# The first scale and shift of an AdaLN block: from rows that are folded and turned to channels made at once

## The chip, the core and the metric

The kernel runs on one core of a Trainium2 chip. The metric is the device time of one execution in microseconds. The kernel before was run three times and takes 1318.79 us in the median (1311.11 to 1322.47).

## What is computed

The reference is one transformer block with adaptive layer norm: a conditioning vector `c` of each of four batch entries makes six vectors of 512 channels, which scale, shift and gate two branches. The first branch is a gated delta rule (a linear attention with a short convolution), the second a gated feed-forward. Everything is float32, x is 4 x 512 x 512.

```python
mod = (silu(c) @ wmod).reshape(4, 6, 1, 512)          # c: 4 x 512, wmod: 512 x 3072
sa, ca, ga, sb, cb, gb = (mod[:, i] for i in range(6))
ga, gb = (sign(g) * maximum(abs(g), 0.25) for g in (ga, gb))   # sign(0) = 1
h = layernorm(x) * (1 + ca) + sa
x = x + ga * attn(h)      # q, k, v projections, convolutions of 4 taps, delta rule, gate, Wo
h = layernorm(x) * (1 + cb) + sb
x = x + gb * ffn(h)       # silu(h @ w_gate.T) * (h @ w_up.T) @ w_down.T
```

The change concerns only the making of `sa` and `ca` (the first shift and scale, j = 0 and j = 1 in the code).

## The kernel before

The kernel is one function, `adaln_block`, written in a tile framework that schedules the recorded instructions on each engine, allocates buffers by tag, and puts in the semaphores. Activations are kept with channels on the partitions (four blocks of 128 channels, `KD = 4`) and the 512 tokens of one batch entry along the free side, so that a scale and a shift by channel are one number per partition. The work runs batch entry by batch entry: batch 0 first goes through normalisation (`first_normed_t`), keys, queries, values, gates and the delta rule, with the others following behind it, and the feed-forward of each entry is laid beside the delta rule of later ones.

**What happens first.** Two of the six column blocks of `w_mod` are loaded at once: j = 1 (scale) and j = 0 (shift), each a tile `wm` of 128 partitions x 4 x 512 (partition and second index together are the 512 rows of the contraction). Each is loaded in two halves of the contraction, k = 0, 1 by the ACT queue and k = 2, 3 by the SP queue (`early_load`, line 175). SP issues `c_in`, then x of batch 0 in two transfers, then the second halves, then the first key weight. ACT makes `sc_t`, the silu of `c` (line 188). `sc_t` is 32 columns wide with 4 used, the rest zero.

**How scale and shift are made.** `modulation_part` (line 209) takes `sc_t` as the fixed side of the matmul and a whole row of 512 columns of `wm` as the moving side. Each of the four blocks of the contraction writes its own strip of 32 partitions of one PSUM bank `pm` (line 213), so the four partial sums stand one above the other. ACT copies the bank to SBUF (`part`, line 216). `modulation_turned` (line 221) then takes each 128-column block of `part` as the fixed side and `fold`, a matrix of four stacked 32x32 identities, as the moving side: this adds the four strips and puts channels on the partitions, into a slice of the bank `scratch` (line 226). ACT writes it to `mod_t` (line 228), adding 1 for the scale. The other modulation vectors (j = 2 to 5) go the same way later, with DVE in ACT's place.

**How they are used.** `first_normed_t` (line 296) makes the statistics of batch 0 on DVE, normalises the four token chunks in place (line 309), transposes 16 blocks of 128x128 on TensorE into four banks `pxt` (line 313), and applies scale and shift on the way out of PSUM, alternately on ACT (line 320) and DVE (line 318), into `ht`. The first key projection `pp_k` (line 478) and the decay projection `pab` (line 370) read `ht`.

**What sets the order.** Each engine works through its instructions in the recorded order after scheduling. TensorE's order around the change is: the four `pm` matmuls of j = 1, one of j = 0, the four folds of j = 1, three `pm` of j = 0, six transposes, the four folds of j = 0, ten transposes, then `pp_k`. A float32 matmul that isn't a transpose shows as two LDWEIGHTS and two MATMUL records, and is counted so below; a transpose shows as one of each. The PSUM tags are `fill` (three banks), `seq` (three banks) and `scratch` (two banks, used in turns). The three `seq` allocations at the start are the fourth `pxt` bank, then `pm` for j = 1 and for j = 0; `pab` comes next and reuses the first.

Of the kernel before, what the change touches and what calls it, by code (L numbers as in the profile page):

```python
# [9 lines left out]
AF = mybir.ActivationFunctionType  # L10
# [5 lines left out]
P = 128  # L16
B, T, D = 4, 512, 512
# [6 lines left out]
KD = D // P  # L24
# [13 lines left out]
def adaln_block(  # L38
# [23 lines left out]
    vec, act, pool, pe, sp = nc.vector, nc.scalar, nc.gpsimd, nc.tensor, nc.sync  # L62
# [12 lines left out]
    def bank(tag, n, name):  # L75
        return ps.tile([P, 512], F32, tag=tag, bufs=n, name=name)

    def fill(name):
        return bank("fill", 3, name)
# [4 lines left out]
    def prep(n):  # L84


        turn[0] ^= 1
        return scratch[:, :, turn[0], :n]

    def seq(name):  # L90
        return bank("seq", 3, name)
# [13 lines left out]
    sc_t = const.tile([P, KD, S], F32, name="sc_t")  # L105
# [12 lines left out]
    mod_t = const.tile([P, 4, KD, B], F32, name="mod_t")  # L118
    MOD = {0: 0, 1: 1, 3: 2, 4: 3}
# [13 lines left out]
    start = const.tile([P, 2, NT, C + 1], F32, name="start")  # L133
# [37 lines left out]
    early = []  # L171
# [36 lines left out]

    def modulation_part(j, wm):

        pm = (seq if j < 2 else fill)(f"pm{j}")
        for k in range(KD):
            pe.matmul(pm[k * S : (k + 1) * S, :], sc_t[:, k, :], wm[:, k, :], start=True, stop=True)
        part = pa_.tile([P, D], F32, tag="acc", bufs=4, name=f"part{j}")
        if j < 2:
            act.copy(part, pm)
        else:
            vec.tensor_copy(part, pm)
        return part

    def modulation_turned(j, part):
        pt = (prep(KD * B)[:, 0] if j < 2 else fill(f"pmt{j}")[:, : KD * B]).rearrange(
            "p (t b) -> p t b", b=B
        )
        for t in range(KD):
            pe.matmul(pt[:, t, :], part[:, t * P : (t + 1) * P], fold[:, :B], start=True, stop=True)
        if j < 2:
            act.activation(mod_t[:, MOD[j]], pt, AF.Identity, bias=1.0 if j == 1 else 0.0)
        else:
            vec.tensor_scalar_add(mod_t[:, MOD[j]], pt, 1.0 if j == 4 else 0.0)  # L230

    def modulation(j, wm):
        part = modulation_part(j, wm)
        if j in MOD:
            return modulation_turned(j, part)
        pg = fill(f"pmg{j}")[:B, :]
        pe.matmul(pg, fold[:, :B], part, start=True, stop=True)
        val = pa_.tile([P, D], F32, tag="acc", bufs=4, name=f"val{j}")[:B]
        vec.tensor_copy(val, pg)
        mag = pa_.tile([P, D], F32, tag="acc", bufs=4, name=f"mag{j}")[:B]  # L240
        vec.scalar_tensor_tensor(mag, val, -1.0, val, ALU.mult, ALU.max)
        vec.tensor_scalar(val, val, 0.0, 2.0, ALU.is_ge, ALU.mult)
        vec.tensor_scalar_add(val, val, -1.0)
        vec.scalar_tensor_tensor(mag, mag, 0.25, val, ALU.max, ALU.mult)
        pool.dma_start(gate_d[j // 3], mag)
# [23 lines left out]
    for i in range(2):  # L269
# [14 lines left out]
        t = stat.tile([P, H, C], F32, name=f"xs{i}")  # L284
# [6 lines left out]
    def statistics(pool_, xt, mv):  # L291
        st = pool_.tile([P, vec.BN_STATS_DIM], F32, tag="st", bufs=2, name="st")
        vec.bn_stats(st, xt)
        vec.bn_aggr(mv, st)

    def first_normed_t(xts):

        mv = pa_.tile([P, NT, vec.BN_AGGR_DIM], F32, tag="mv", name="mv0")
        rstd = pa_.tile([P, NT], F32, tag="rstd", name="rstd0")
        pts = [(fill if k < 3 else seq)(f"pxt0_{k}") for k in range(KD)]  # L300

        for j, wm in early:
            modulation_turned(j, modulation_part(j, wm))
        for c in range(NT):
            statistics(pa_, xts[c], mv[:, c, :])
        act.activation(rstd, mv[:, :, 1], AF.Sqrt, bias=eps)
        vec.reciprocal(rstd, rstd)
        for c in range(NT):
            vec.tensor_scalar(
                xts[c], xts[c], mv[:, c, 0:1], rstd[:, c : c + 1], ALU.subtract, ALU.mult  # L310
            )
            for k in range(KD):
                pe.transpose(pts[k][:, c * P : (c + 1) * P], xts[c][:, k * P : (k + 1) * P], ident)
        ht = pa_.tile([P, KD, T], F32, tag="ht", bufs=3, name="ht0")
        for k in range(KD):
            shift, scale = (mod_t[:, i, k, 0:1] for i in range(2))
            if k % 2:
                vec.tensor_scalar(ht[:, k, :], pts[k], scale, shift, ALU.mult, ALU.add)
            else:
                act.activation(ht[:, k, :], pts[k], AF.Identity, bias=shift, scale=scale)  # L320
        return ht
# [642 lines left out]


    hts, xts = {0: first_normed_t(xts)}, {}
    keys([0], hts)
    rest = list(range(1, B))
# [93 lines left out]
```

## Time and profile before

| What | Value |
|---|---|
| Runs before, median (lowest to highest) | 1318.79 us (1311.11 to 1322.47) |
| Execution that was profiled, its own time | 1315.23 us |
| Span of its trace | 1313.5 us, 18027 instructions |
| TensorE matmul busy (PE) | 1242.2 us, 95% |
| TensorE weight load busy (PEld, overlaps PE) | 777.2 us, 59% |
| DVE / ACT / POOL busy | 713.9 / 386.3 / 249.3 us |
| First `pm` matmul | 5.50 us after the start |
| First `ht` activation | 20.32 us |
| First `pp_k` matmul | 21.14 us |

The times are microseconds from the start of the span. A row of a group of instructions reads: line, engine, operation, output <- inputs, shapes, count, and then durations. Matmuls are pipelined: each is listed from its start to its end, and neighbours overlap, so the rate of a row of matmuls is the distance between their starts and not the length of one. The chain of waits is followed back from the last instruction, at each step to what released it.

### The profile page before, as it was taken

Reading aid. Unit: us, or ns where it says so; the run is one execution under the profiler, and the core shown is the slowest. Engines: PE = TensorE matmul, PEld = TensorE weight load, DVE = VectorE, ACT = ScalarE, POOL = GpSimd, SP = SyncE. Lnnn points to the kernel's source line nnn. Section 1 sums busy time; section 2 is a strip of 40 time slices with the busy share of each in tenths; the row PEclk is TensorE's granted clock in tenths of the full one; section 3 lists DMA queues with packets and bytes.
Section 4 is the critical chain, followed back from the end, with each engine's and each line's share of the span. In section 5 each row is a group of like instructions: output and inputs, shape, how many; then the busy total and the mean of one; then the engine's idle time right before and its main releaser. Section 6 shows DMA issues by size and latency. Waiting matters only on the chain.

```text
span 1313.5 us, 18027 instructions
## 1 busy us (share of the span) xinstructions
PE 1242.2 (95%) x6620; PEld 777.2 (59%) x6620; DVE 713.9 (54%) x1547; ACT 386.3 (29%) x740; POOL 249.3 (19%) x299
## 2 busy tenths in 40 slices
PE   6899898899999998989999999899999999999998
PEld 3444355444444565757757666676666577576665
DVE  4767765555288245774445558644464444444443
ACT  3643346643142344211103332110234211011110
POOL 4210223543200012020021121011111201111111
PEclk9889999999999999999999999899999999999999
DMA  5979647767955447664335455443622243354331
GB/s 154 267 186 285 200 119 227 186 213 225 276 165 161 118 108 184 204 178 134 126 115 163 124 124 164 134 144 101 185 78 71 94 144 116 117 189 143 117 112 64
DMA packets 213271, 204.06 MB, mean 155 GB/s; under 512 B 95032, under 2 KB 163640, under 8 KB 213184
## 3 DMA queue, kind: packets, MB, share of 16 engines
q1 hardware_dynamic: 191408, 167.14, 44.6%
q0 software_dynamic: 4096, 20.99, 4.2%
q10 hardware_dynamic: 17680, 14.78, 3.5%
q8 instruction: 53, 0.87, 0.3%
q14 instruction: 34, 0.28, 0.1%
HBM read 152.94 MB, written 46.78 MB: 152 GB/s over the span
## 4 chain that ended last, share of the span: by engine, by line
PE 66%; DVE 13%; DMA 9%; POOL 4%; issue 3%; ACT 2%; SPq 1%; POOLq 0%; ACTq 0%; DVEq 0%
PE phg L927 15%; PE pd L899 15%; PE phu L927 11%; PE pwo L803 5%; PE pp_v L478 3%; PE pp_g L478 2%; PE pm L762 2%; DVE ti L660 2%; DVE tip L656 2%; PE scratch L689 2%; DMA wsum<-wsu 1%; PE pf L753 1%; DMA wsum<-wsg 1%; PE pp_k L478 1%; DMA wsg<-in_w_gate_t_dram 1%
## 5 line engine op out<-in xcount | busy, mean ns | idle before, releaser
L899 PE MATMUL pd<-wdn,hid 128*128 128x512 f32 x512 | 225.5, 593 | 0.0
L905 POOL TENSOR_TENSOR xm<-xm,tmpf 128x512 f32<-128x512 f32 x64 | 81.3, 1270 | 451.9 <-DVE tmpf L904 451.9
L899 PEld LDWEIGHTS pd<-wdn,hid 128*128 128x128 f32 x512 | 97.7, 191 | 109.2 <-issue 102.6
L927 PE MATMUL phg<-hf,wg 128*128 128x256 f32 x512 | 138.6, 388 | 0.3 <-DMA wg<-wsum 0.3
L927 PEld LDWEIGHTS phg<-hf,wg 128*128 128x128 f32 x512 | 96.4, 193 | 21.4 <-issue 7.3
L927 PE MATMUL phg<-hs,wg 128*128 128x256 f32 x384 | 103.4, 389 | 4.4 <-DVE hid L934 4.3
L927 PE MATMUL phu<-hf,wu 128*128 128x256 f32 x384 | 99.9, 384 | 2.1 <-DMA wu<-wsum 2.0
L904 DVE TENSOR_TENSOR tmpf<-pd,gb 128x512 f32<-128x512 f32 x64 | 44.1, 689 | 104.0 <-PE pd L899 93.0
L927 PE MATMUL phu<-hs,wu 128*128 128x256 f32 x384 | 96.1, 384 | 3.5 <-DVE up L940 3.5
L478 PE MATMUL pp_v<-ht,wv 128*128 128x512 f32 x192 | 93.6, 632 | 4.5 <-DVE v L561 2.3
L932 ACT COPY hid<-phg 128x256 f32<-128x256 f32 x32 | 11.9, 371 | 288.8 <-PE phg L927 286.5
L803 PE MATMUL pwo<-wo,ot 128*128 128x512 f32 x192 | 93.3, 617 | 0.0
L478 PE MATMUL pp_g<-ht,wg 128*128 128x512 f32 x192 | 91.4, 618 | 1.6 <-issue 1.6
L927 PEld LDWEIGHTS phu<-hs,wu 128*128 128x128 f32 x384 | 72.4, 191 | 22.0 <-DVE up L940 9.0
L927 PEld LDWEIGHTS phg<-hs,wg 128*128 128x128 f32 x384 | 71.6, 194 | 18.3 <-DVE hid L934 5.8
L927 PEld LDWEIGHTS phu<-hf,wu 128*128 128x128 f32 x384 | 71.3, 191 | 15.0 <-issue 5.2
L478 PEld LDWEIGHTS pp_v<-ht,wv 128*128 128x128 f32 x192 | 36.9, 202 | 46.2 <-issue 43.4
L488 DVE SCALAR_TENSOR_TENSOR acc_v<-pp_v,conv_v,acc_v 128x511 f32<-128x511 f32 (+2 forms) x72 | 53.3, 743 | 8.8 <-ACT acc_v L486 8.1
L478 PEld LDWEIGHTS pp_g<-ht,wg 128*128 128x128 f32 x192 | 35.1, 195 | 38.2 <-issue 37.0
L956 ACT ACTIVATE hid<-hid 128x1024 f32<-128x1024 f32 x32 | 33.8, 1057 | 79.9 <-DVE hid L940 63.5
L762 PE MATMUL pm<-r,l 128*128 128x128 f32 x384 | 52.7, 283 | 1.0 <-ACT r L758 0.8
L803 PEld LDWEIGHTS pwo<-wo,ot 128*128 128x128 f32 x192 | 34.4, 192 | 30.1 <-issue 28.3
(236 smaller groups left out, 1812.8 us busy)
## 6 DMA issues: line engine op xcount, KB each, us to landing
wdn<-in_w_down_t_dram SPq DMA_DIRECT2D x32, 512.0 KB, 4.3
wg<-wsum SPq DMA_DIRECT2D x32, 512.0 KB, 3.7
wu<-wsum SPq DMA_DIRECT2D x32, 512.0 KB, 3.6
wg<-wsum SPq DMA_DIRECT2D x32, 384.0 KB, 4.3
wu<-wsum SPq DMA_DIRECT2D x32, 384.0 KB, 4.4
wsum<-wsg POOLq DMA_DIRECT2D x8, 896.0 KB, 4.0
wsum<-wsu POOLq DMA_DIRECT2D x8, 896.0 KB, 4.5
wg<-in_w_g_dram SPq DMA_DIRECT2D x24, 256.0 KB, 3.2
```

The costliest lines, as they stand in the source:

```text
L478: pe.matmul(pp, w[:, k, :], ht[:, k, :], start=(k == 0), stop=(k == KD - 1))
L488: vec.scalar_tensor_tensor(acc[:, i:], pp[:, : T - i], taps[:, col, TAPS - 1 - i : TAPS - i], acc[:, i:], ALU.mult, ALU.add,)
L656: vec.tensor_tensor(v, pm[:, j, j + 1 :, None].broadcast_to([n, m, j]), t[:, j : j + 1, :j].broadcast_to([n, m, j]), ALU.mult,)
L660: vec.tensor_add(t[:, j + 1 :, :j], t[:, j + 1 :, :j], v)
L689: pe.matmul(pv[:, u, 2 * par : 2 * par + 2, :], kc[i][us, p, par : par + 2, :], qc[i][us, p, par : par + 2, :], start=True, stop=True,)
L762: pe.matmul(pm[:, h], l[:, hs.start + h, 2 * par : 2 * par + 2, :], r[:, par, hs.start + h], start=True, stop=True,)
L803: pe.matmul(pw, ot[:, h, :], wo[:, h, :], start=(h == 0), stop=(h == H - 1))
L899: pe.matmul(pd, hids[q, i // 2][:, i % 2, c * P : (c + 1) * P], wdn[q, i // 2][:, i % 2, :], start=(i == 0), stop=(i == NQ - 1),)
L904: vec.tensor_mul(tmp, pd, gb)
L905: pool.tensor_add(xm[c], xm[c], tmp)
L927: pe.matmul(o, l[:, k], r[:, k], start=k == 0, stop=k == 1)
L956: act.activation(hid, hid, AF.Silu)
```

## The change

Scale and shift are no longer made as rows, copied, folded and turned. For each block of 128 output channels the 128x128 block of `wm` is the fixed side and the four used columns of `sc_t` are the moving side, so the result has channels on the partitions at once, 128 x 4 for each block, and the contraction is summed in PSUM. This is done by halves of the contraction in the order in which they are loaded: first half of the scale, first half of the shift, second half of the scale, second half of the shift, eight matmuls each. The results go straight to `mod_t` by ACT. The later modulation vectors keep the old way; their branches for j < 2 are dropped from the two functions.

```diff
     def modulation_part(j, wm):
-        pm = (seq if j < 2 else fill)(f"pm{j}")
+        pm = fill(f"pm{j}")
         for k in range(KD):
             pe.matmul(pm[k * S : (k + 1) * S, :], sc_t[:, k, :], wm[:, k, :], start=True, stop=True)
         part = pa_.tile([P, D], F32, tag="acc", bufs=4, name=f"part{j}")
-        if j < 2:
-            act.copy(part, pm)
-        else:
-            vec.tensor_copy(part, pm)
+        vec.tensor_copy(part, pm)
         return part
 
     def modulation_turned(j, part):
-        pt = (prep(KD * B)[:, 0] if j < 2 else fill(f"pmt{j}")[:, : KD * B]).rearrange(
-            "p (t b) -> p t b", b=B
-        )
+        pt = fill(f"pmt{j}")[:, : KD * B].rearrange("p (t b) -> p t b", b=B)
         for t in range(KD):
             pe.matmul(pt[:, t, :], part[:, t * P : (t + 1) * P], fold[:, :B], start=True, stop=True)
-        if j < 2:
-            act.activation(mod_t[:, MOD[j]], pt, AF.Identity, bias=1.0 if j == 1 else 0.0)
-        else:
-            vec.tensor_scalar_add(mod_t[:, MOD[j]], pt, 1.0 if j == 4 else 0.0)
+        vec.tensor_scalar_add(mod_t[:, MOD[j]], pt, 1.0 if j == 4 else 0.0)
...
     def first_normed_t(xts):
...
-        for j, wm in early:
-            modulation_turned(j, modulation_part(j, wm))
+
+        pms = [seq(f"pmt{j}")[:, : KD * B].rearrange("p (t b) -> p t b", b=B) for j, _ in early]
+        for k in (0, KD // 2):
+            for (j, wm), pt in zip(early, pms):
+                for t in range(KD):
+                    for i in range(k, k + KD // 2):
+                        pe.matmul(
+                            pt[:, t, :], wm[:, i, t * P : (t + 1) * P], sc_t[:, i, :B],
+                            start=(i == t == 0), stop=(i == t == KD - 1),
+                        )
+                if k:
+                    act.activation(mod_t[:, MOD[j]], pt, AF.Identity, bias=1.0 if j == 1 else 0.0)
```

In the changed program TensorE's order is the 32 new matmuls in the order above, then the 16 transposes without a break, then `pp_k` as before. ACT's order is the same less the two copies; the orders of DVE, POOL and SP are the same.

## The prediction

> **What bounds the kernel now.** I read the page first, then the chain of waits over the first 60 us, then the instructions of the tiles that the change touches, and last the granted clock by stretches. On the page TensorE leads the chain that ends last:
>
> ```profile
> PE 66%; DVE 13%; DMA 9%; POOL 4%; issue 3%; ACT 2%; SPq 1%; POOLq 0%; ACTq 0%; DVEq 0%
> ```
>
> The change lies in the first 21 us. There the chain of waits (start, length, what; both in us) runs through every piece that is edited:
>
> ```profile
> 2.35 8.23 DMA wm<-in_w_mod_dram
> ...
> 10.62 1.95 PE pm L213 x5
> ...
> 12.59 0.59 ACT part L216
> ...
> 13.32 1.84 PE scratch L226 x8
> 15.16 1.86 PE pm L213 x6
> 17.02 1.47 PE pxt L313 x6
> 18.49 0.90 PE scratch L226 x8
> 19.39 0.94 PE pxt L313 x8
> 20.34 0.77 ACT ht L320
> ...
> 21.14 1.98 PE pp_k L478 x4
> ```
>
> So a microsecond won or lost before 21.14 us is one on the chain. After it nothing in the chain waits for a fixed moment: the loads it meets later (x from 37.48 to 42.21) are issued behind finished activations, so they move along. The weights for the first projections landed early enough: SP issued the last of them at 14.55 us, they land some 4.4 us after issue, and the timeline shows it idle between 15.6 and 26.96 us. I pass the shift at 21.14 to the end one to one.
>
> The second view is the landing of the four half blocks of `w_mod` (issue rows, then issue to landing):
>
> ```profile
> L179 ACTq DMA_DIRECT2D wm<-in_w_mod_dram x2: 493/512/532, 0.8 to 1.3; - x2
> L179 SPq DMA_DIRECT2D wm<-in_w_mod_dram x2: 614/750/886, 2.4 to 3.3; - x2
> DMA to landing us min/median/max: 4.5/7.6/8.7
> ```
>
> The scale's first half landed at 0.8 + 4.5 = 5.3; the ACT queue's median of 5.7 puts the other of its two at 6.9, so the shift's first half came at 1.3 + 6.9 = 8.2. The second halves came at 10.58 (the chain) and at 3.3 + 8.7 = 12.0.
>
> The third view is the price of one load-and-multiply step, from two windows of the fold into `scratch` (start 13.2 to 15, then after 18.3) and two of the transposes:
>
> ```profile
> L226 PEld LDWEIGHTS scratch<-fold,part x8: 285/333/334, 13.3 to 14.7; 128*128 128x128 f32 x8
> L226 PE MATMUL scratch<-fold,part x8: 344/354/355, 13.3 to 14.8; 128*128 128x4 f32 x8
> ...
> L226 PE MATMUL scratch<-fold,part x7: 252/253/354, 18.4 to 19.1; 128*128 128x4 f32 x7
> ...
> L313 PE MATMUL pxt<-ident,xt x6: 421/421/477, 16.9 to 18.1; 128*128 128x128 f32 x6
> ...
> L313 PE MATMUL pxt<-ident,xt x10: 272/272/306, 19.2 to 20.3; 128*128 128x128 f32 x10
> ```
>
> The same instruction takes 354 ns before and 253 ns after some 18.5 us. The clock records begin at 18.60 us and say full speed from there; the column PEclk prints 1.00 before them too, but the durations show that TensorE ran at the lower clock until then. Eight steps of the fold took 1.84 us, so their spacing at the lower clock is (1.84 - 0.354) / 7 = 0.212 us; ten transposes at the full one took 1.29 us, (1.29 - 0.272) / 9 = 0.113 us. Both load 128 columns per step, and the moving side hardly counts.
>
> The fourth view asks what raises the clock (columns: stretch, its length, then busy time of PE, PEld, DVE, ACT, POOL, granted clock, DMA share, GB/s; the two rows below are the timeline's):
>
> ```profile
> 45.91:49.32 3.41, 3.41 (x20) 2.10 (x20) 2.67 (x7) 1.31 (x3) 0.41 (x2) 0.50 1.13 193
> 49.32:52.73 3.41, 3.41 (x5) 1.33 (x4) 1.39 (x3) 0.26 (x1) 0.54 (x1) 0.50 1.20 240
> ...
> 45.94 1.02 PE L504 MATMUL pn_k<-sel,sq_k 128*64 128x2 f32 x16
> 46.90 2.92 PE L478 MATMUL pp_q<-ht,wq 128*128 128x512 f32 x3
> ```
>
> The clock changes on a grid of 3.41 us. The stretch from 45.91 had TensorE busy throughout, but 1.02 us of it with matmuls of two moving columns, and the clock stayed at one half; the next, all 512-column matmuls, was followed by full speed at 52.73. Weight loading with almost nothing streamed does not seem to count.
>
> **The change, part by part.** *Removed:* 16 steps of `pm` (8 matmuls of two passes), 16 of the fold, and the two ACT copies to `part` (0.59 us each, the first on the chain). From 10.62 to the 13th transpose, whose end starts `ht`, the old chain spends 9.7 us. *Added:* 4 groups of 8 matmuls, two passes each as in the fold, so 64 steps, each a 128x128 load and four moving columns: the form of the fold row exactly. The instruction orders of DVE, POOL and SP are the same before and after; ACT loses only the copies. The two result banks are again two of the three `seq` banks, and `pab` reuses the same first one. The wait for `ident` moves to the first transpose, and POOL made that by 1.7 us. The two `mod_t` activations (0.18 us) remain; the last comes some 2.5 us before `ht`, hidden behind the transposes, and would cost 0.18 without that cover. DVE's normalised rows are done at 13.98, which is no limit below.
>
> Now the sum at the lower clock. The first group starts, as `pm` did, at 5.47 us. Each group is 16 x 0.212 = 3.4 us: ends at 8.9, 12.3, 15.6 and 19.0. No half block is late (8.2 against 8.9, 10.6 against 12.3, 12.0 against 15.6), so TensorE waits nowhere, which is why its own rate sets the time and earlier data buy nothing. Queued behind the groups are the 16 transposes, and DVE and ACT wait for these. The 13th starts at 19.0 + 12 x 0.212 = 21.6 and ends 0.42 later, 22.0; `ht` takes 0.77 and the issue gaps 0.06: the first projection starts at 22.85 instead of 21.14, +1.7 us.
>
> Next the clock. If it is raised at 22.01, the next line of the old grid, this is all. The stretch 18.60 to 22.01 would hold 3.0 us of transposes (88%); against it, in the old run 15.19 to 18.60 had 3.1 us of wide matmuls and transposes (91%) and was followed by the raise, while 45.91 with some 70% was not. If it comes one line later, at 25.43, the projections run at half rate for 2.6 us: 1.3 us more, +3.0. Neither row decides, and 88% is nearest the one that raised it, though the grid's phase need not repeat, so I take the middle: **+2.4 us**. The page's execution took 1315.23 us by its own time (span 1313.5), which gives 1317.6; the median of the runs shown is 3.6 us higher, which gives 1321.2, rounded to **1321**.
>
> [...]
>
> **Rivals.** *The groups raise the clock.* For it: they occupy TensorE without a gap from 5.47 us, and the stretch before 18.60 that raised it held 0.5 us of folds. Against it: 45.91, and the stretch 11.77 to 15.19, where 1.8 us of folds did not raise it (though with an idle gap of 0.77). By the grid, 8.36 to 11.77 would be the first full stretch: 30 steps done, 34 left at 0.113, end at 15.6; the 13th transpose starts at 17.0, ends at 17.2, and the projection begins at 18.05: -3.1 us, 1315.7 by the median. With a kinder phase the bound is the last landing, 12.0 + 16 x 0.113 = 13.8, or -5.
>
> *The shift is lost.* The kernel has eleven more spells of half clock between 45.9 and 831 us, 51 us together, each costing half its length. Moving all work against the grid by 2 us can add or drop one or two of 3.41 us (1.7 us each), and swallow the change: 1318.8. For it: three runs of one kernel spread over 11.4 us. Against it: nothing in the chain soaks it up by itself. To move the time by over 1% (13.2 us, about what a measurement of this kernel can tell from no change) eight such spells would have to come or go; a small chance on either side.
>
> *The steps don't overlap.* All eight matmuls of a group add into few columns, two by two into the same four. If each step had to finish before the next began, it would cost 0.333 + 0.354 = 0.69 us, 64 of them 44 us, ending at 49.4 instead of 19.0: +33 us in all, 1352. It decides from 0.38 us per step on, where the whole loss passes 13.2 us. Against it: in the fold, two passes into the same four columns already follow at 0.212.
>
> **How the numbers follow.** The lower clock throughout the groups 0.67; the groups raise it 0.17; shift lost 0.09; steps that don't overlap 0.03; clock spells beyond 1% 0.04, split evenly. The time is the first case's. The range takes in -5 at the low side and +3.0 at the high side about the median, and some 4 us of run spread, which the low run (1311) and the high run (1322) show: 1312 to 1327. Within 1%: the first three, less 0.03 for spread at the edges, 0.90. Slower: 0.03 + 0.02 + 0.01 = 0.06. Faster: 0.02 + 0.02 = 0.04.
>
> **What would show it.** Right: the new matmuls run from 5.5 to about 19 us in an even row, 0.21 apart, without a wait for `w_mod` beyond the first; matmul length 354 ns; the first `pp_k` near 22.9; the first clock record at 21.5 or later. Wrong: steps of 0.11 us before 15 us and a clock record near 12 (first rival), a gap in the row before the third or fourth group, or a `pp_k` start after 30 us.

## The result and the profile after

The changed kernel takes 1324.05 us in the median, the kernel before on the same chip 1318.04: a ratio of 1.0048 [1.0029, 1.0068]. It is half a per cent slower; the forecast was 1321 and "within 1%". The profiled execution of after took 1323.99 us (span 1322.3), that of before 1315.23 (span 1313.5).

The chain of waits of after, first 30 us (start, length, what; in us), and the two rows of the tile `pmt` (count, min/median/max in ns, first and last start, shape):

```profile
0.81 4.24 DMA c_in<-in_c_t_dram
5.06 0.22 ACT sc_t L188
5.29 0.09 issue
5.38 13.78 PE pmt L300 x64
19.16 2.89 PE pxt L315 x13
...
22.14 0.79 ACT ht L322
...
22.97 2.09 PE pp_k L480 x4
```

```profile
L300 PEld LDWEIGHTS pmt<-sc_t,wm x64: 285/333/333, 5.3 to 18.7; 128*128 128x128 f32 x64
L300 PE MATMUL pmt<-sc_t,wm x64: 343/354/355, 5.4 to 18.8; 128*128 128x4 f32 x64
```

The 64 steps are one unbroken piece, 13.78 / 64 = 0.215 us each, with no wait for a half of `w_mod` inside it: the chain no longer holds the 8.23 us of `wm<-in_w_mod_dram` and begins with the load of `c_in` and `sc_t`. A weight load takes 333 ns to the last step, as in the slow fold of before (192 once the clock was raised), so the lower clock lasted through all of them; the first clock record of after stands at 23.22 us. The first projection starts at 22.97 instead of 21.14 (+1.83). By the first `pat` (the fold of the decay projection, a few matmuls behind) it is 26.95 against 25.02.

At the end the profiled pair is 8.8 us apart, though. The engines' shares of the chain on the page hardly differ (66% TensorE before):

```profile
PE 67%; DVE 13%; DMA 9%; POOL 4%; issue 4%; ACT 2%; SPq 1%; POOLq 0%; ACTq 0%; DVEq 0%
```

So the start came out as forecast against the page of before, and what had to be explained was the rest.

### The profile page after: what moved, and what is told of

It reads as the page before. It is cut to its first block, busy times and chain, and to the rows that moved or that the text cites. A ratio compares the mean times of both kernels' runs of the same rounds, so it can differ in the third digit from the quotient of the medians.

```text
span 1322.3 us, 18088 instructions
## 1 busy us (share of the span) xinstructions
PE 1253.8 (95%) x6652; PEld 792.8 (60%) x6652; DVE 712.2 (54%) x1547; ACT 385.5 (29%) x738; POOL 249.5 (19%) x299
## 4 chain that ended last, share of the span: by engine, by line
PE 67%; DVE 13%; DMA 9%; POOL 4%; issue 4%; ACT 2%; SPq 1%; POOLq 0%; ACTq 0%; DVEq 0%
PE pd L901 14%; PE phg L929 14%; PE phu L929 11%; PE pwo L805 5%; PE pp_g L480 4%; PE pp_v L480 3%; PE pm L764 2%; DVE ti L662 2%; PE scratch L691 2%; DVE tip L658 2%; PE pp_k L480 2%; PE pf L755 1%; PE scratch L734 1%; DVE acc_v L490 1%; PE pmt L300 1%
## 5 line engine op out<-in xcount | busy, mean ns | idle before, releaser
L764 PEld LDWEIGHTS pm<-r,l 128*128 128x128 f32 x384 | 49.6, 200 | 8.3 <-ACT r L760 3.5
```

Of the source, the lines that this page charges most:

```text
L764: pe.matmul(pm[:, h], l[:, hs.start + h, 2 * par : 2 * par + 2, :], r[:, par, hs.start + h], start=True, stop=True,)
```

## The experiments

Ratios are to the kernel before on the same chip, with 95% intervals. "Growth" is measured in the traces: how much later DVE's, ACT's and GpSimd's instructions come, counted from the first `pat`, than in the profiled run of before, at 210 to 220 us behind `pat` less the same at 160 to 170 us (the median over the instructions there).

**1. The kernel before, once more.** No edit.

> The kernel before, unchanged, for the spread of its runs and for a second trace. The traces so far put 1.9 us of the 8.8 us between the two profiled executions before the first key projection, and 6.8 us into spells of half clock after it (51 us of them in the trace of before, 65 us of after). Theory that the later spells are more often met by the changed kernel: ratio 1.000 within 0.002, and a mean granted clock near 0.980 over its runs, against 0.9768 over the 19 runs of the changed one (0.003 of 1320 us is 4 us of half clock, 2 us of time). Theory that the later spells were luck of the two profiled executions: the same mean clock of 0.977 here, so that the 6 us between the medians must lie before the first record of the clock. The first raise of the clock need not come at 18.6 us again: if the grid lies otherwise, at 22 to 26 us.

Ratio 0.9986 [0.9962, 1.0011]; growth -0.3 us. The mean granted clock of its runs is 0.982, that of the runs of the changed kernel 0.977, so the later spells of half clock were not just luck of the two profiled executions. But its start isn't that of the page. From the timeline of this run (start, length, engine, line, what):

```profile
18.25 1.71 PE L226 MATMUL scratch<-fold,part 128*128 128x4 f32 x8
19.82 2.37 PE L313 MATMUL pxt<-ident,xt 128*128 128x128 f32 x10
22.48 3.07 PE L478 MATMUL pp_k<-ht,wk 128*128 128x512 f32 x4 [0.29 <-ACT ht L320]
...
27.44 0.97 PE L386 MATMUL pat<-fold,ab 128*128 128x32 f32 x8
```

The last ten transposes take 2.37 us here and took 1.29 on the page: the clock was raised at 24.69 us, not at 18.60. The page of before, from which I had 21.14, had an early line of the clock's grid (the clock records of that trace, all but the last, which the end of the trace cuts off, are 3.41 us long or multiples of it). A third trace of the same work (experiment 7) has `pp_k` at 22.43 and `pat` at 26.70. Against the mean `pat` of these three, 26.4, four traces of the changed kernel and its repeats (26.95, 26.90, 27.71, 27.87) stand at 27.4: the start costs about 1.0 us, not 1.9.

**2. Do weight loads raise the clock?** The moving side of the groups is repeated 32 times, to 128 columns; the weights and the number of steps stay.

```diff
-  pms = [seq(f"pmt{j}")[:, : KD * B].rearrange("p (t b) -> p t b", b=B) for j, _ in early]
+  pms = [seq(f"pmt{j}").rearrange("p (t n b) -> p t n b", n=S, b=B) for j, _ in early]
...
-      pt[:, t, :], wm[:, i, t * P : (t + 1) * P], sc_t[:, i, :B],
+      pt[:, t], wm[:, i, t * P : (t + 1) * P],
+      sc_t[:, i, None, :B].broadcast_to([P, S, B]),
...
-      act.activation(mod_t[:, MOD[j]], pt, AF.Identity, bias=1.0 if j == 1 else 0.0)
+      act.activation(mod_t[:, MOD[j]], pt[:, :, 0], AF.Identity, bias=1.0 if j == 1 else 0.0)
```

> The changed kernel, with the four moving columns repeated 32 times to 128, so that each step still loads 128 columns and now streams 128 as well; the extra results are not read. Theory that only streamed columns raise the clock: the steps stay 0.21 us apart until the first line of the grid behind a full stretch of 3.41 us, between 8.8 and 12.3 us, then fall to 0.11 us; the groups end at 14 to 16 us instead of 19.2, and the first key projection starts at 17 to 19 us instead of 22.97: 4 to 6 us less than the changed kernel, about 3 less than before, ratio 0.996 to 0.999. Theory that the clock follows the time since TensorE began, whatever it streams: no change, first raise at 22 us or later, ratio 1.004 to 1.006. Theory that a step costs by its streamed columns: 128 columns for four make it slower, ratio above 1.01.

The scheduler also moved the gates' exponential and `pab` ahead, so a second version ties that exponential's scale to a small tile `one` that DVE makes behind `ht`; ACT, GpSimd and SP then keep the changed kernel's order, and only `pab` stays ahead of `pp_k`. A third version repeats only 8 times, to 32 columns, and needs no such tile. The second is shown against the changed kernel, the third against the first version.

```diff
-            act.activation(neg_a, neg_a, AF.Exp)
+            one = pa_.tile([P, 1], F32, tag="one", bufs=1, name="one")
+            vec.tensor_scalar(one, hts[0][:, KD - 1, 0:1], 0.0, 1.0, ALU.mult, ALU.add)
+            act.activation(neg_a, neg_a, AF.Exp, scale=one)
```

```diff
-  pms = [seq(f"pmt{j}").rearrange("p (t n b) -> p t n b", n=S, b=B) for j, _ in early]
+  pms = [seq(f"pmt{j}")[:, : KD * 8 * B].rearrange("p (t n b) -> p t n b", n=8, b=B) for j, _ in early]
...
-      sc_t[:, i, None, :B].broadcast_to([P, S, B]),
+      sc_t[:, i, None, :B].broadcast_to([P, 8, B]),
```

> The wide-sided variant again. There the scheduler, expecting wider matmuls to take longer, had put the exponential of neg_a and its table load ahead of the first ht activations, and moved parts of the first key and query stages; here that exponential takes its scale from a tile of ones that DVE makes behind ht (one more DVE instruction of about 0.2 us), so ACT, SP and POOL have the order of the changed kernel again, and only pab stays ahead of pp_k. Theory that this reordering ate the 4 to 6 us that the wide side won at the start: ratio 0.9950 to 0.9975. Theory that the gain is lost later whatever the order: 0.9985 to 1.0010, as the wide side had.

> The changed kernel with 32 moving columns (the four, eight times) instead of 4 or 128; the order on all engines is that of the changed kernel. A step streams for about a quarter of the time that its load of 128 columns takes. Theory that the clock follows the share of time in which columns stream: a quarter is too little, the steps stay 0.21 us apart, first raise at 22 us or later, first key projection at 23.0, ratio as the changed kernel. Theory that any real streaming is enough: first raise between 8.8 and 12.3 us, first key projection at 17 to 19 us, ratio 0.995 to 0.998.

The rows of `pmt` in the second version, then in the third:

```profile
L300 PEld LDWEIGHTS pmt<-sc_t,wm x64: 186/192/333, 5.5 to 14.1; 128*128 128x128 f32 x64
L300 PE MATMUL pmt<-sc_t,wm x64: 272/275/553, 5.5 to 14.2; 128*128 128x128 f32 x64
```

```profile
L300 PEld LDWEIGHTS pmt<-sc_t,wm x64: 288/333/338, 5.3 to 18.7; 128*128 128x128 f32 x64
L300 PE MATMUL pmt<-sc_t,wm x64: 390/401/402, 5.4 to 18.8; 128*128 128x32 f32 x64
```

With 128 columns most loads take 192 ns: the clock was raised at 8.79 us in the first version (8.39 in the second), the groups end at 14.4 (14.5), and `pp_k` starts at 18.4 (18.5), some 4.5 us earlier than in after. Two more traces with 128 columns, of experiments 7 and 8, have the raise at 11.43 and 10.74 us. With 32 columns all 64 are at the lower clock, as with four, the raise is at 23.79, and the ratio is 1.0053 [1.0024, 1.0082]. A pass of 512 columns takes 0.88 us at the lower clock (six of `pp_q` from 46.90 to 52.17 us in before), so by estimate 32 columns stream for 0.055 us, a quarter of a step of 0.215, and 128 for 0.22, all of it. The loads and the number of steps are the same in all of these, so what raised the clock early is what is streamed; the first rival of the prediction is out for this change. But the gain didn't arrive: 0.9997 [0.9972, 1.0022] for the first version and 0.9999 [0.9969, 1.0029] for the second, whose order of instructions was kept, so the reordering isn't what ate it. Growth is +3.0 and +2.5 us, and +3.1 with 32 columns.

**3. The order of the loops.** Scale wholly first, then shift.

```diff
-  for k in (0, KD // 2):
-      for (j, wm), pt in zip(early, pms):
+  for (j, wm), pt in zip(early, pms):
+      for k in (0, KD // 2):
```

> The changed kernel with its four groups in another order: both halves of the scale, then both of the shift. Theory that the groups are bound by their own 0.212 us steps and that the order by landing only avoids a wait: the first group ends at 8.8 us, the second waits for its block until 10.6, and everything behind is 1.8 us later, the groups ending near 20.9 and the first key projection starting near 24.7 us, against 22.97. Theory that the landings don't matter at all: no gap, 22.97 us.

A miss: the scheduler put the four groups back into the changed kernel's order (the scale's `mod_t` is still written at 15.9 us, behind the third group, and the 64 steps have no gap), so this is the changed kernel again and tells nothing of the order. One execution took 1323.57 us, `pp_k` at 23.07, growth +2.7 us.

**4. The changed kernel, once more.**

> The changed kernel, unchanged, beside the kernel before on the same chip. In the first traces the two kernels differ before the first key projection by 1.8 us (22.97 against 21.14), but the second trace of before has 22.48, with the clock raised at 24.69 instead of 18.60, so over many grid positions the starts would differ by about 1 us or less. Theory that the start is all: ratio 1.0003 to 1.0015 and the same mean granted clock as the runs of before (0.980). Theory that the changed kernel also meets more half clock later: ratio 1.003 to 1.007 and a mean clock near 0.977, 0.003 below the runs of before on this chip.

Ratio 1.0065 [1.0040, 1.0090], `pp_k` at 23.03, growth +2.2 us (3.6 in the first trace). The loss is no matter of one chip, and the mean clock, 0.978 against 0.980 for before on this chip, is lower again.

**5. Is a delay at the start passed on?** The kernel before with its 16 transposes made twice; in the second version with the order kept as in 2.

```diff
-            for k in range(KD):
+            for k in range(2 * KD):
+                k %= KD
```

> The kernel before, with each of the 16 transposes of batch 0 made twice, a pure delay of the start by wide enough matmuls that shouldn't lower the clock: 16 steps of 0.11 us at full clock, 0.21 at half, so 1.8 to 3.4 us at the first key projection. Theory that a later start is passed on one to one and the spells of half clock fall by chance: ratio 1.0013 to 1.0026, mean clock as in the kernel before. Theory that any later start makes TensorE meet more half clock spells behind it: ratio 1.0045 or more with a mean clock lower by 0.002 or more than in the kernel before.

> The kernel before with each of the 16 first transposes made twice, and the exponential of neg_a held behind ht as in the wide variant in order, so that ACT, SP and POOL keep the order of before and only pab stands ahead of pp_k. A pure delay of about 2 to 3.4 us at the start. Theory that a later start is passed on one to one, and that the 6 us of the first version came in part from the reordering: ratio 1.0015 to 1.0027, mean clock as the runs of before. Theory that a later start is amplified behind it: ratio 1.004 to 1.007.

1.0047 [1.0022, 1.0073] and 1.0042 [1.0013, 1.0071], with `pat` at 30.13 and 28.20, 3.7 and 1.8 us behind the mean of before. A delay ahead of `pat` isn't swallowed. Both ratios lie where a delay that is amplified behind the start was expected to put them (5.5 and 6.2 us for a delay of 1.8 to 3.7 us). But both intervals reach down to one to one, and the mean clock is only 0.001 below that of before; which of the two holds stays open. Growth is +2.4 us in the first and +0.3 in the second: it doesn't go with the delay.

**6. Where the growth sits.** It is in all six traces with the new groups so far, whatever their start. Comparing events one by one puts it at three loads of feed-forward weights that SP issues in quarters, `wsg`, `wsu` and `wsg`, and that GpSimd adds up before it can go on to `xr`, the sum behind the first branch (DVE and TensorE wait for that). One of them is on the chain of waits, in before and in after:

```profile
229.71 4.62 DMA wsg<-in_w_gate_t_dram
...
234.49 0.73 POOL wsg L866
...
237.40 1.24 POOL xr L806
```

```profile
236.18 5.61 DMA wsg<-in_w_gate_t_dram
...
241.95 0.73 POOL wsg L868
...
244.85 1.23 POOL xr L808
```

The same load takes 5.61 us instead of 4.62. What made loads slower, in a part that the change doesn't touch?

**7. First theory: places in SBUF.** As the two `part` tiles are gone, the allocator puts the four buffers of tag `acc` 64 bytes further on and uses them in another turn. Two small tiles of that tag ahead of the groups undo the first; the same was done to the wide kernel and to the kernel before.

```diff
+        for j in range(2):
+            vec.memset(pa_.tile([P, D], F32, tag="acc", bufs=4, name=f"gap{j}")[:1, :1], 0.0)
```

> Two small tiles of tag `acc` (one element of each set to zero on VectorE) are allocated before the groups, so that the `acc` buffers lie in the same place of SBUF as in the kernel before; all else is the changed kernel. Place theory: the part of the loss that sits between 154 and 217 us behind `pat` (later landings of the wsg/wsu loads) comes from the 64 bytes by which those buffers moved, so it is 0 +- 0.4 us there against before, and the ratio is 1.000 to 1.0025, what is left being the start. Rival (the loss there comes from the start's timing against the loads, or from the clock): growth there of 2.2 to 3.7 us as in all runs of the changed kernel so far, ratio 1.005 to 1.0065.

> The changed kernel with 128 moving columns in the groups (early raise of the clock) and with the two small `acc` tiles ahead. Place theory: it keeps the 4 to 6 us gained at the start and loses the growth behind it: ratio 0.995 to 0.9975, first raise before 10 us, pp_k near 18.4 us. Rival: as the wide kernel so far, 1.000, with 2.2 to 3.0 us of growth between 154 and 217 us behind `pat`.

> The kernel before with the same two small tiles ahead: the base of the `acc` buffers stays where it was, and which of the four a tile gets moves on by two. Place theory by the base: 1.000, no growth behind `pat`. Place theory by the slot (which of the four buffers is in use when): 1.003 with 2 to 3.7 us between 154 and 217 us behind `pat`. Rival without places: 1.000 and no growth.

1.0033 [1.0010, 1.0057] with growth +1.9 us; 0.9989 [0.9960, 1.0018] with +1.6; 0.9992 [0.9966, 1.0018] with -0.1. The growth stays where the groups are new and stays away from before: the theory falls. The intervals alone would have left it half alive (1.0033 lies between both expectations); the growth in the trace, -0.1 against 1.6 and 1.9, decides. The wide kernel's raise came at 11.43 us and its `pp_k` at 19.65 here, later than the expected 10 and 18.4.

**8. Second theory: the fetches of TensorE's own program.** The page of after counts instructions and the queue that brings them (packets, MB, share):

```profile
PE 1253.8 (95%) x6652; PEld 792.8 (60%) x6652; DVE 712.2 (54%) x1547; ACT 385.5 (29%) x738; POOL 249.5 (19%) x299
...
q8 instruction: 53, 0.87, 0.3%
```

53 packets of 0.87 MB are 16.4 KB each. TensorE's records in the trace, waits included, are 13,632: 257 for each packet. From the start of one packet to the next TensorE starts 256 of them on the mean (168 to 336), in before 255 (176 to 324), so I take the packets for the fetches of its program. The old way has 32 matmuls and 32 weight loads fewer and one wait more (13,569 records), so by these counts a fetch of after should come 63 instructions earlier in TensorE's work from the first `pat` on. Now the queues in the time of that load on the chain, from the start of its last issue to its landing, first in before and then in after (the columns are queue, packets, MB, share of 16 engines):

```profile
q1 hardware_dynamic: 1223, 1.20, 96.6%
```

```profile
q1 hardware_dynamic: 1701, 1.31, 99.6%
q8 instruction: 1, 0.02, 1.1%
```

A fetch has moved into the load. The larger number of q1 packets in after is no rival: in the first 4.5 us behind the last issue they are 1186 in before and 1187 in after, and only the longer wait takes in more. Over all fourteen traces it looks so (time from the start of the last issue of a load to GpSimd's first addition; loads named by their time behind `pat`):

| Load | Traces with a fetch early in it | Traces without |
|---|---|---|
| `wsg`, 178 us | all eight with the new groups and no empty steps, fetch 0.6 to 1.3 us after the last issue: 3.65 to 4.08 us | six: 2.45 to 2.83 us |
| `wsu`, 193 us | three (fetch at 1.1 to 1.5 us): 4.36 to 5.45 us | the others, none or later than 2.4 us: 2.66 to 3.64 us |
| `wsg`, 207 us | eight (fetch at 0.0 to 3.3 us): 5.38 to 6.92 us | six: 4.59 to 4.87 us |

The six without a fetch in the first load are the three of before, the two with doubled transposes and the last run, told below. The other transfers that start around the first load are the same in all fourteen (a read of `sg` 0.57 us behind the last issue, one of `kc` at 1.08), and the write of `kd` that only the slower ones also meet starts at 3.4 us or later, when the fetch is over. Even the growth of +2.4 in experiment 5 fits: in that trace a fetch fell into the third load (6.21 us). A fetch packet took 0.88 to 1.44 us in the first 360 us of before, the size of the delay in the first load (about 1.2 us); the third is delayed by 0.5 to 2.3 us, and why by so much is not shown. In the second load the fetch isn't all: without an early one it takes 3.44 to 3.64 us with the new groups and 2.66 to 2.94 with the old.

To test it, the wide kernel in order got 96 empty steps (one weight column, one moving column) ahead of the groups, while TensorE still waits for its first inputs: 192 more instructions, so 255 more than before, nearly one whole fetch. In the two traces the work of DVE, ACT, GpSimd and SP has the same order.

```diff
+        nil = eps.bitcast(mybir.dt.bfloat16)[:, :1]
+        for _ in range(96):
+            pe.matmul(pms[0][:1, 0, 0, :1], nil, nil, start=True, stop=True)
         for k in (0, KD // 2):
```

> The wide kernel in the changed kernel's order (wide_in_order) with 96 steps of one weight column and one moving column ahead of the groups, written into a result element that the groups then overwrite: 192 more TensorE instructions. In the traces so far TensorE's instructions come in fetches of 16 KB (queue 8), one for each 257 instructions on the mean; every changed kernel has 63 more instructions ahead of the first `pat` than the kernel before, and its fetch falls 178.5 to 178.9 us behind `pat` (less its own shift), in the middle of a wsg load that lands at about 180; in the kernel before and with the 16 transposes made twice it falls at 181.3 to 183. With 192 more it is back at the kernel before's place. Fetch theory: fetch at 181.5 to 183.5, growth between 154 and 217 us behind `pat` 0 +- 0.5 us (wide_in_order had +2.5), and the ratio 0.996 to 0.998 if the 96 steps fit into the wait for w_mod (up to 4.2 us from 1.2 us on; at 40 ns a step they do, at 84 ns, as for 4 weight columns, the groups start 3.7 us later and the ratio is 0.999 to 1.001). Rival (the fetch only happens to lie there): growth 1.6 to 3.0 us as in the other wide kernels, ratio 0.999 to 1.002.

Ratio 0.9927 [0.9896, 0.9958], 1308.42 us: faster than both kernels. That is more than the expected 0.996 to 0.998. The empty steps end well before the groups can start (timeline; the last row is of the weight loads):

```profile
1.24 2.54 PE L298 MATMUL pmt<-eps 128*1 128x1 bf16 x96 [1.24 <-POOL sel L121]
5.43 10.16 PE L303 MATMUL pmt<-sc_t,wm 128*128 128x128 f32 x64 [1.65 <-ACT sc_t L188]
...
9.28 6.12 PEld L303 LDWEIGHTS pmt<-sc_t,wm 128*128 128x128 f32 x48 [0.40 <-DMA wm<-in_w_mod_dram]
```

The wait in the last row is new, and it is the same effect once more: a fetch now starts at 6.82 us and takes 0.98, and the shift's first half of `w_mod` lands at 9.24 us instead of the 8.25 of the wide kernel in order.

The later fetch is at 182.2 us behind `pat` counted on the scale of before (there 182.0; 178.6 in the wide kernel in order). The load on the chain in the wide kernel in order (the piece of its chain of waits, then the queues in its time), and then the same two of this one:

```profile
224.69 5.22 DMA wsg<-in_w_gate_t_dram
```

```profile
q1 hardware_dynamic: 1466, 1.26, 96.3%
q8 instruction: 1, 0.02, 1.2%
```

```profile
225.74 4.49 DMA wsg<-in_w_gate_t_dram
```

```profile
q1 hardware_dynamic: 1194, 1.19, 93.6%
```

5.22 us with a fetch in it, 4.49 without; the first load takes 2.45 us instead of 3.66, and growth is +0.6 instead of +2.5. The empty steps touch neither the loads nor GpSimd, only the place of the fetches, so I take the fetches as shown to be the cause of the growth in the first and third load. The 0.6 lies just over the expected 0.5; the second load, at 3.26 us, isn't quite as short as in before (2.75). The traces don't show the 0.7% itself: the profiled execution of this kernel (1311.81 us) was among the slowest of its ten, and that of the wide kernel in order took 1310.00. Nor does a pair of traces show how much of a growth reaches the end: between 350 and 600 us behind `pat`, traces that had fallen behind that of before come back by up to 6.9 us. For that the means over many runs are needed.

**The sum.** Each run comes with its mean granted clock, which splits its time (means; before is the runs of experiments 1 to 8 that stood beside the others, on four chips):

| Kernel | Runs | Time | Time x clock | Time x (1 - clock) |
|---|---|---|---|---|
| before, four chips | 103 | 1315.2 | 1289.2 | 26.0 |
| after, two chips | 29 | 1323.0 | 1292.6 | 30.3 |
| 128 columns (three versions) | 36 | 1314.4 | 1287.1 | 27.3 |
| 128 columns and 96 empty steps | 10 | 1307.5 | 1285.0 | 22.5 |

The third column of numbers (time x clock) is what would be left at full clock, the last what the spells of half clock cost if each costs half its length. That is an estimate from the passes of 512 columns in before (0.88 us each in such a spell, 0.43 outside); no run tests it over the whole time. By chip, time x clock of before runs from 1288.5 to 1290.4, so a difference of a microsecond says little. After loses 3.4 us there, which is about the start (1.0) and the growth (2.2 to 3.6). The wide kernels should gain 4.0 at the start (`pat` at 22.4 on the mean) and give back 1.6 to 3.0, and show 2.1. The last version should show some 2.3 (`pat` at 23.44, growth 0.6) and shows 4.2, which isn't explained.

In the last column after has 4.3 us more than before, the last version 3.5 less. The traces tell where some of it lies: from 190 to 240 us behind `pat`, where GpSimd waits for the later of the three loads, TensorE ran at half clock for 3.4, 6.8 and 3.4 us in the traces of before, for 6.8 to 20.5 (mean 10.7) in the eight with new groups and no empty steps, and for 3.4 again in the last version. So the moved fetches and the spells go together there. It isn't shown that the one makes the other: the second version of experiment 5 has 10.2 us there without a fetch in the first or third load, and over whole runs the wide kernels have 27.3 and the changed kernel with its buffers moved back 26.9, only about one more than before, with the same colliding fetches. This half of the loss stays open.

## Why the prediction was right, and where it was wrong

- *The price of a step and of the groups: right.* 0.215 us against 0.212; end of the groups 19.16 against 19.0; `pp_k` at 22.97 against 22.85; no wait for a half of `w_mod`; first clock record at 23.22, "at 21.5 or later" (21.97 to 24.98 in four traces, so taking the middle between 22.01 and 25.43 was fair). The row of the fold told all this.
- *The groups don't raise the clock: right*, and for the reason given from the stretch at 45.91 us. The runs add a bound: 13.8 us of back-to-back steps of four columns didn't raise it, as many steps of 32 columns didn't either (raise at 23.79 us), and steps of 128 columns did, 2.8 to 6.0 us after the first of them in four traces.
- *Steps that don't overlap: out.* 0.215 us a step.
- *The base of the sum: wrong.* I took 21.14 from one execution as the start of before. Its clock was raised at 18.60; two more traces had `pp_k` at 22.48 and 22.43. I noted that the grid's phase need not repeat for after, and didn't apply it to before. Against the mean of three starts the term "+2.4 us" was some 1.0 us.
- *"I pass the shift at 21.14 to the end one to one": the step that failed.* Nothing soaked the shift up (experiment 5), but the way to the end added to it: 2.2 to 3.6 us of growth in the two traces of after, mostly from fetches that moved into loads, and some 4.3 us of half clock by the means, whose cause is open. The second rival had named such spells, one or two of them to be added or dropped; here the equal of two or three was added. I had looked at the orders on five engines and at the loads, and counted TensorE's 64 added and 32 old matmuls only for their time. That they also move the fetches (the one at the first load from 182.0 us behind `pat` in before to 178.6 in the wide kernel in order) I could have asked of the row of queue 8 on the page of before, which I didn't use.
- *The result.* +6 us measured against +2.4 forecast. The start was priced 1.4 us too high and the way behind it at nothing, where it cost some 5 us; that the time still lies in the range of 1312 to 1327 is owed to the width taken for run spread and in part to luck, not to the sum.

## What to carry to other kernels

Before explaining a loss far from an edit, compare two traces from a common event onward, load by load, and look at every queue in the time of the slower load, the instruction fetches too: here 63 more TensorE instructions moved a fetch by some 3.4 us (182.0 to 178.6 us behind `pat`) into a load, and a version with 96 empty steps in idle time ran 0.7% faster than before where the same kernel without them ran even with it (0.9999). Steps that load 128x128 weights took more moving columns for nothing here: 0.21 us apart at the lower clock with 4, 32 and 128 columns, and 128 raised the clock some 11 to 17 us earlier. A start that runs before the first clock record should be priced from several executions, since it moved by 1.3 us between two runs of one kernel (`pp_k` at 21.14 and 22.48) whose clock was raised at 18.60 and at 24.69 us.

## What the runs showed of the hardware that I had not expected

- One 16 KB instruction fetch inside a load of four 128 KB quarters delayed its use by about 1.2 us (2.45 to 2.83 us without, 3.65 to 4.08 us with one, `wsg` at 178 us), though such fetches are 0.3% of the time of the DMA engines.
- Empty bf16 steps of one weight column and one moving column cost 2.54 / 96 = 0.026 us each ahead of the first raise of the clock, where a 128-column float32 load-and-multiply step costs 0.215.
- 64 back-to-back steps of 4 or 32 moving columns left the lower clock in place for 13.8 us (weight loads of 333 ns in the median, 192 once it was raised); with 128 columns the clock was raised at 8.4 to 11.4 us in four traces.
